# A two-layer spectral and convolution kernel: where the mix's matrix S is made, and how its operands are prepared

## The chip, the core and the metric

The kernel runs on one core of one Trainium2 chip. The metric is the device time of one execution in microseconds (us). The core has a matrix engine (TensorE, "PE", with its weight loads listed apart as "PEld"), a vector engine (VectorE, "DVE"), a scalar engine (ScalarE, "ACT"), GpSimd ("POOL") and SyncE ("SP"), which here only issues DMA transfers. The engines have their own instruction streams, taken in order, and wait for each other by semaphores. Operands lie in SBUF (128 partitions, also called lanes here); matmuls write to PSUM[...].

## The reference

Layer 0 is a Laplace neural operator on x (16 images, 16 channels, 256 x 256); layer 1 a small convolution network. Only layer 0's frequency part is touched:

```python
alpha = jnp.fft.fft2(x, axes=(-2, -1))
A = 1.0 / (omega1[:, None, None, None] - weights_pole1[None])
Bm = 1.0 / (omega2[:, None, None, None] - weights_pole2[None])
S = jnp.einsum('ikpq,oikp,xikq->oxik', weights_residue, A, Bm)
output_residue1 = jnp.einsum('biox,oxik->bkox', alpha, S)
...
x1 = jnp.fft.ifft2(output_residue1, s=(Ny, Nx), axes=(-2, -1)).real
```

S holds, for each of 256 x 256 frequencies (o, x), a complex 16 x 16 matrix from input channel i to output channel k. It factors: first sum over q with Bm (it depends on x only), then over p with A (it depends on o). Since x is real, only the row frequencies o = 0 to 128 are needed.

## The kernel before

The program has four stages, one after the other: `layer0_forward` (the transform of x, and beside it the making of tables), `layer0_mix` (the product with S, and the inverse transform along x), `layer0_back` (the inverse transform along y), and `layer1`.

**The forward stage** goes through 64 steps: 16 images (b) with 4 groups of 4 channels (cg). A step computes `rows` twice (16 matmuls into pu, L207, and 16 into pv, L214; the results leave PSUM through ACT's `right` L222 and DVE's `u` L224), then `poles` (L241), and from the second image on two or three calls of `columns` for the image before: each has two PSUM tiles px of 16 matmuls (L313), copied out by ACT (L320) and stored to `al` from GpSimd's queue (L329). Group norm's mean and variance are two tiny matmuls a step (L34, L42). The PSUM pools: psu 2 banks for pu, psv 2, psd 1, psx 2 for px, psn 1[...]. PE's order is written out by hand; the other engines' order is set by the scheduler.

At the end of each step from the fifth on (`i >= 4`), the generator `tables` is advanced by one piece. It makes three tables and stores them to DRAM from SyncE's queue: `td`, the sum over q (16 pieces: 6 DVE instructions for Bm, 8 for the weights, 4 matmuls L437 into a px bank, a copy L445 by ACT); `avd`, the values of A for each of the 33 groups of four row frequencies (11 pieces of three groups, 9 DVE instructions each, L466 to L490); and `ed`, exponentials for the back stage (16 pieces of some 25 DVE instructions and a sine on ACT, L515 to L536 and L769 to L783).

**The mix stage** goes through 33 groups g of four row frequencies; PE, ACT, DVE and POOL are ordered by hand. For a group:

- `poles` (L629, 6 DVE instructions) spreads the loaded A into block form `lt`; `residues` (L643) makes S: 16 k x 2 v x 2 h matmuls of `tt` (all of td, resident in SBUF) with `lt`, and copies each k from PSUM into `s` (L651 on DVE, L653 on ACT, half each). `s` is laid out [partition = (f, i), x, v, k], so these copies write elements that lie 64 bytes apart.
- `expand` (L605 on ACT, L607 on DVE) multiplies the loaded spectrum `alc` with one of four masks into `alb` [partition, x, j, b]; 16 instructions of 1024 elements a group (6 on ACT, 10 on DVE), writing elements 512 bytes apart.
- `mix` (L665) does 8 chunks of 32 small products, each chunk copied out of PSUM into `y` by ACT (L672). Four PSUM banks (psg) are for this and for `residues`.
- for each of the four frequencies f: `turn` (8 transposes L681, copied out as `yt` by DVE L687 and ACT L685) and `columns` (32 matmuls L700 into two banks `ph`; ACT copies the odd part L709, DVE adds and subtracts L712 and L713 to `h`, GpSimd issues the stores to `hd` L720). Between `turn` and `columns` of f stand four k of `residues` for the next group and a share of `expand`. `columns` of f = 3 is put off and runs in two halves between the chunks of the next group's `mix`.

`s`, `lt` and `alb` have one buffer each; the spectrum has four buffers of a quarter each, loaded by SyncE (L595) for the group after next as soon as a quarter has been expanded.

Of the kernel before, what the change touches and what calls it, by code (L numbers as in the profile page):

```python
# [10 lines left out]
F32 = mybir.dt.float32  # L11
# [61 lines left out]
def layer0_forward(ctx, tc, d, al, bd, tabs):  # L73
# [262 lines left out]
    with tc.manual_schedule(engines={mybir.EngineType.PE}):  # L336
# [4 lines left out]
        pieces = tables(ctx, tc, d, psx, tabs)  # L341
        acc = rsc = None
        for i, (b, cg) in enumerate(steps):
# [16 lines left out]
            if b:  # L360
                for g0 in range(8 * cg, 8 * cg + 8 if cg < 3 else NF, 4):
                    columns(b - 1, g0, rsc)
            if i + 2 < len(steps):
                fetched.append(fetch(*steps[i + 2]))
            if i >= 4:
                next(pieces, None)
# [16 lines left out]
def tables(ctx, tc, d, psum, tabs):  # L383

    nc = tc.nc
    td, avd, ed = tabs
# [3 lines left out]

    krow = load(nc, cp, d["krow_t"], [P, N], "krow_t")
    w = frequencies(nc, cp, d["tx"], krow, [P, N], "wt")
# [18 lines left out]
    for k in range(C):  # L411
        e = tp.tile([P, N], F32, tag="te", name="te")
        r = tp.tile([P, N], F32, tag="trec", name="trec")
        br = tp.tile([P, N], F32, tag="tbr", name="tbr")
# [7 lines left out]
        for h in range(2):  # L422
            wt = tp.tile([P, 2, 2, 16, M], F32, tag=f"wt{h}", name="wt")
            shape = [P, 16, M]
            for part, c, coef in ((0, 0, rr), (0, 1, ri), (1, 0, nri), (1, 1, rr)):
                nc.vector.tensor_tensor(
                    wt[:, part, c],
                    mt[:, h].unsqueeze(2).to_broadcast(shape),
                    coef[:, k].unsqueeze(1).to_broadcast(shape),
                    ALU.mult,  # L430
                )
            wts.append(wt)
        yield
        ps = psum.tile([P, 2, N], F32, tag="px", name="pt")
        for h, wt in enumerate(wts):
            for part, rhs in ((0, br), (1, e)):
                nc.tensor.matmul(  # L437
                    ps[:, h],
                    lhsT=wt[:, part].rearrange("p c i m -> p (c i m)"),
# [4 lines left out]
        t = tp.tile([P, 2, N], F32, tag="tt", name="tt")  # L444
        nc.scalar.copy(t, ps)  # L445
        nc.sync.dma_start(out=td[:, :, k], in_=t)

    krow = load(nc, cp, d["krow_m"], [P, N], "krow_m")  # L450
    w = frequencies(nc, cp, d["ty"], krow, [P, N], "wm")
    sign = load(nc, cp, d["sign_m"], [P, 1], "sign_m")
    pr = cp.tile([P, 32], F32, name="tpr")
    pi = cp.tile([P, 32], F32, name="tpi")
    for q in range(4):
        nc.sync.dma_start(out=pr[32 * q : 32 * q + 32], in_=d["p1r_ip"])
        nc.sync.dma_start(out=pi[32 * q : 32 * q + 32], in_=d["p1i_ip"])
    nc.vector.tensor_scalar(pi, pi, sign, None, ALU.mult)
    pr2 = cp.tile([P, 32], F32, name="tpr2")
    nc.vector.tensor_tensor(pr2, pr, pr, ALU.mult)  # L460
    npr = cp.tile([P, 32], F32, name="tnpr")
    nc.vector.tensor_scalar(npr, pr, -1.0, None, ALU.mult)
    for g in range(NF):
        four = [P, 32, 4]
        e = tp.tile(four, F32, tag="ae", name="ae")
        nc.vector.tensor_tensor(  # L466
            e,
            w[:, 4 * g : 4 * g + 4].unsqueeze(1).to_broadcast(four),
            pi.unsqueeze(2).to_broadcast(four),
            ALU.add,  # L470
        )
        r = tp.tile(four, F32, tag="ar", name="ar")
        nc.vector.tensor_tensor(r, e, e, ALU.mult)
        nc.vector.tensor_tensor(r, r, pr2.unsqueeze(2).to_broadcast(four), ALU.add)
        nc.vector.reciprocal(r, r)
        av = tp.tile([P, 32, 4, 3], F32, tag="av", name="av")
        half = [64, 32, 4]
        nprb = npr.unsqueeze(2)
        nc.vector.tensor_tensor(av[:64, :, :, 1], r[:64], nprb[:64].to_broadcast(half), ALU.mult)
        nc.vector.tensor_tensor(av[64:, :, :, 1], r[64:], e[64:], ALU.mult)  # L480
        nc.vector.scalar_tensor_tensor(
            av[:64, :, :, 0].rearrange("p k f -> p (k f)"),
            e[:64].rearrange("p k f -> p (k f)"),
            -1.0,
            r[:64].rearrange("p k f -> p (k f)"),
            ALU.mult,
            ALU.mult,
        )
        nc.vector.tensor_tensor(av[64:, :, :, 0], r[64:], nprb[64:].to_broadcast(half), ALU.mult)
        nc.vector.tensor_scalar(av[:, :, :, 2], av[:, :, :, 0], -1.0, None, ALU.mult)  # L490
        nc.sync.dma_start(out=avd[g], in_=av.rearrange("p k f l -> p (k f l)"))
        if g % 3 == 2:
            yield


    phase = load(nc, cp, d["phase"], [P, 1], "phase")
    turn = cp.tile([P, 1], F32, name="turn")
    nc.vector.tensor_scalar(turn, phase, TWO_PI, None, ALU.mult)
    last = load(nc, cp, d["last"], [P, 1], "last")
    c1 = 6.28125  # L500
    c2 = float(np.float32(TWO_PI - c1))
    for i, axis in enumerate("12"):
        pr = cp.tile([P, C], F32, name=f"epr{axis}")
        pi = cp.tile([P, C], F32, name=f"epi{axis}")
        for a in range(2):
# [1028 lines left out]
```

## Time and profile before

Three runs took 7180.24, 7201.38 and 7224.01 us (median 7201.38). The profiled execution took 7223.74 us, with a span of 7222.0 us between its first and last instruction.

| row of the profile | count | mean ns |
| --- | --- | --- |
| L437 PE, first factor of S | 128 | some 400 |
| L445 ACT copy tt, 128 x 512 from PSUM | 16 | 585 |
| L418 DVE reciprocal, 128 x 256 | 16 | 1742 |
| L518 DVE tensor_scalar, 128 x 512 in SBUF | 16 | 418 |
| L605 ACT expand, 128 x 1024 | 198 | 2055 |
| L607 DVE expand, 128 x 1024 | 330 | 1397 |
| L651 DVE, L653 ACT copies of S, 128 x 512 | 264 each | 1023, 1028 |
| L672 ACT copy y, L685 ACT copy yt | 264, 129 | 587, 586 |
| L536 SyncE store of ed, 256 KB | 16 | 338 (median) |
| L329 GpSimd store of al | 544 | 608 |

In the profile's lines, "out<-in" are the names of the tiles, "x2048" is a count, the numbers after the bar are the busy time of the whole group in us and the mean of one instruction in ns, and after the next bar stands the idle time of that engine just before these instructions and what ended it. Matmuls are pipelined, so a group's busy time divided by its count is what one costs, while its mean is from start to end. The clock (PEclk) is the share of full speed that TensorE was granted.

### The profile page before, as it was taken

Reading aid. Unit: us, or ns where it says so; the run is one execution under the profiler, and the core shown is the slowest. Engines: PE = TensorE matmul, PEld = TensorE weight load, DVE = VectorE, ACT = ScalarE, POOL = GpSimd, SP = SyncE. Lnnn points to the kernel's source line nnn. Section 1 sums busy time; section 2 is a strip of 40 time slices with the busy share of each in tenths; the row PEclk is TensorE's granted clock in tenths of the full one; section 3 lists DMA queues with packets and bytes.
Section 4 is the critical chain, followed back from the end, with each engine's and each line's share of the span. In section 5 each row is a group of like instructions: output and inputs, shape, how many; then the busy total and the mean of one; then the engine's idle time right before and its main releaser. Section 6 shows DMA issues by size and latency. Waiting matters only on the chain.

```text
span 7222.0 us, 144350 instructions
## 1 busy us (share of the span) xinstructions
PE 6585.2 (91%) x55592; PEld 3670.2 (51%) x55592; DVE 5553.1 (77%) x10106; ACT 3882.2 (54%) x6043; POOL 3517.7 (49%) x4614
## 2 busy tenths in 40 slices
PE   7889999889999999899789999999999999999996
PEld 5677778666666666677533333333333333333331
DVE  8999985466666666688688777878878787787875
ACT  2223333456656666222376666666666666666662
POOL 2334455322222222566664666556666566665563
PEclk9989999999999999999899999999999999999998
DMA  3444444433333333899878898898988888988886
GB/s 100 115 114 124 120 123 128 121 92 99 100 98 99 100 96 87 288 326 326 272 211 243 250 266 261 251 263 251 273 258 250 258 256 261 264 256 258 257 259 218
DMA packets 716081, 1443.39 MB, mean 200 GB/s; under 512 B 98954, under 2 KB 525254, under 8 KB 673638
## 3 DMA queue, kind: packets, MB, share of 16 engines
q1 hardware_dynamic: 567206, 959.76, 44.7%
q0 software_dynamic: 148192, 474.40, 21.9%
q8 instruction: 444, 7.27, 0.4%
q14 instruction: 239, 1.96, 0.1%
HBM read 877.12 MB, written 556.47 MB: 199 GB/s over the span
## 4 chain that ended last, share of the span: by engine, by line
PE 38%; DMA 7%; ACT 3%; DVE 1%; SPq 1%; issue 1%; POOL 0%; DVEq 0%; POOLq 0%; ACTq 0%
PE c2ps L1185 14%; PE c L1037 11%; PE pd L1105 11%; DMA rows<-cf 5%; ACT wide L1085 2%; DMA z<-zn 2%; PE pr L1064 2%; SPq L1017 0%; DVE top L1116 0%; ACT r L1073 0%; ACT L1240 0%; ACT L1085 0%; POOL o L1253 0%; DVE t L1113 0%; DVE pair L1175 0%
## 5 line engine op out<-in xcount | busy, mean ns | idle before, releaser
L1085 ACT ACTIVATE wide<-c,b 32x512 f32<-32x512 f32 x2176 | 1479.5, 680 | 295.1 <-PE c L1037 246.3
L1116 DVE TENSOR_TENSOR top<-pd,t 32x512 f32<-32x512 f32 x2176 | 1504.2, 691 | 55.6 <-DMA cf<-top 3.1
L1113 DVE TENSOR_TENSOR t<-pd,r 64x512 f32<-64x512 f32 x1088 | 744.4, 684 | 517.6 <-PE pd L1105 495.1
L1037 PE MATMUL c<-z,w 102*128 102x512 f32 x2048 | 1017.7, 629 | 122.9 <-ACT wide L1085 100.9
L1097 POOL COPY wide<-wide 32x1031 f32<-32x1031 f32 (+1 forms) x576 | 575.4, 999 | 1007.9 <-ACT wide L1085 980.5
L1105 PE MATMUL pd<-wide,dw 128*128 128x512 f32 x2048 | 993.4, 607 | 12.5 <-DVE top L1116 11.0
L720 POOL DMA_DIRECT2D hd<-h x512 | 324.3, 640 | 1206.8 <-DVE h L713 1182.0
L1185 PE MATMUL c2ps<-rows,c 128*32 128x512 f32 x6144 | 743.3, 617 | 100.8 <-DMA rows<-cf 96.1
L1037 PEld LDWEIGHTS c<-z,w 102*128 102x128 f32 x2048 | 377.8, 195 | 725.4 <-issue 475.5
L1105 PEld LDWEIGHTS pd<-wide,dw 128*128 128x128 f32 x2048 | 382.0, 192 | 573.8 <-issue 427.8
L1098 POOL COPY wide<-wide 32x1031 f32<-32x1031 f32 (+1 forms) x576 | 581.6, 1010 | 33.7
L1056 ACT ACTIVATE bot<-c,b 128x512 f32<-128x512 f32 x544 | 344.4, 684 | 470.7 <-issue 382.2
L700 PE MATMUL ph<-ix,yt 64*128 64x256 f32 x4128 | 505.3, 392 | 7.8 <-issue 7.1
L643 PE MATMUL ps<-tt,lt 128*64 128x256 f32 x4224 | 496.1, 385 | 13.1 <-DMA tt<-td 9.2
L1185 PEld LDWEIGHTS c2ps<-rows,c 128*32 128x32 f32 x6144 | 178.2, 110 | 622.5 <-issue 394.1
L313 PE MATMUL px<-wxn,u 128*64 128x256 f32 x4224 | 482.4, 380 | 7.9 <-ACT o L320 7.8
L207 PE MATMUL pu<-fy,eo 128*128 128x128 f32 x2048 | 425.7, 291 | 25.3 <-DVE u L224 21.1
L700 PEld LDWEIGHTS ph<-ix,yt 64*128 64x128 f32 x4128 | 395.1, 191 | 95.1 <-issue 47.2
L873 POOL TENSOR_TENSOR x<-x,o 128x512 f32<-128x512 f32 x256 | 324.4, 1267 | 217.8 <-DVE o L872 216.3
L607 DVE TENSOR_SCALAR alb<-alc,m 128x1024 f32<-128x1024 f32 x330 | 420.0, 1397 | 0.0
L214 PE MATMUL pv<-at,eo 128*128 128x128 f32 x2048 | 412.5, 285 | 0.0
L651 DVE COPY s<-ps 128x512 f32<-128x512 f32 x264 | 265.4, 1023 | 190.1 <-PE ps L643 172.5
(217 smaller groups left out, 11707.6 us busy)
## 6 DMA issues: line engine op xcount, KB each, us to landing
rows<-cf SPq DMA_DIRECT2D x128, 2176.0 KB
z<-zn SPq DMA_DIRECT2D x768, 257.8 KB
cf<-top POOLq DMA_DIRECT2D x512, 240.0 KB, 6.9
cf<-bot POOLq DMA_DIRECT2D x96, 840.0 KB, 11.6
alc<-al SPq DMA_DIRECT2D x264, 256.0 KB
zn<-zb SPq DMA_DIRECT2D x128, 516.0 KB
o<-zn SPq DMA_DIRECT2D x128, 516.0 KB
z<-in_x SPq DMA_DIRECT2D x64, 1024.0 KB
```

Of the source, the lines that this page charges most:

```text
L207: nc.tensor.matmul(pu[:, xh, e].rearrange("p v m -> p (v m)"), lhsT=lhs, rhs=fy[:, e], start=True, stop=True,)
L313: nc.tensor.matmul(ps[64 * k : 64 * k + 64, :, h], lhsT=u[:, h, part, g0 + j + k].rearrange("p f c -> p (f c)"), rhs=wxn[:, h, part], star ...
L643: nc.tensor.matmul(ps[64 * h : 64 * h + 64, v], lhsT=lt[:, h, k, 1 - v : 3 - v].rearrange("p l f c -> p (l f c)"), rhs=tt[:, h, k], start= ...
L700: nc.tensor.matmul(ph[q][:, e], lhsT=yt[lanes, i].rearrange("p t k -> p (t k)"), rhs=ix[lanes, i], start=n == 0, stop=n == 3,)
L1037: nc.tensor.matmul(ps[:, a], lhsT=w, rhs=z[:k, c : c + 2, 0:N], start=True, stop=True)
L1085: nc.scalar.activation(self.feat[64 - 32 * q : 96 - 32 * q, f, self.groups[g], :H], ps[q][32 * f : 32 * f + 32], AF.Mish, bias=b1[0][32 * ...
L1097: nc.gpsimd.tensor_copy(flat[0:32, f, 1:m], flat[64:96, f, 0 : m - 1])
L1098: nc.gpsimd.tensor_copy(flat[96:128, f, 0 : m - 1], flat[32:64, f, 1:m])
L1105: nc.tensor.matmul(ps, lhsT=dwt if self.tail else dw, rhs=self.feat[:, f, cs, :H], start=True, stop=True,)
L1113: nc.vector.tensor_tensor(t[64:128], ps[:64], self.r[:, cs], ALU.mult)
L1116: nc.vector.tensor_tensor(self.top[32 * f : 32 * f + 32, cs, q], ps[lanes], t[lanes], ALU.add)
L1185: nc.tensor.matmul(ps[32 * j : 32 * j + 32], lhsT=w[:, blk], rhs=src[:, 4 * j + blk : 4 * j + blk + 4, x : x + H], start=(i, blk) == (0, 0 ...
```

## The change

It moves the whole of S's making into the forward stage. `tables` now has two interleaved parts. `residues` takes the 16 k in pairs: `first` makes the sum over q as before (now kept in SBUF as `tt`); `second` makes A for 8 input channels and all 132 row frequencies at once (6 DVE and 8 ACT instructions) into `a`; `products` (16 groups of row frequencies at a time) and `last_products` (the last group) multiply the two by matmuls of 32 rows, in four PSUM banks, two from psx and two from psu; `evict` copies each bank to one of three SBUF buffers on ACT, and a store to the new DRAM table `sd` is issued from ACT's queue. The exponentials are as before, spread between. There are 128 pieces instead of 43; one is taken after the first `columns` of each step (and after g0 = 28), one at each step's end, from the second image on.

In the mix `poles`, `residues`, `tt`, `lt` and `avd` are gone. S of a group is loaded as `raw`, twice: as stored (v = 0) and with its two halves swapped (v = 1), three buffers of 2 MB. `prepare` makes `s` and `alb` for a range of 32 column frequencies. The spectrum is one tile of 2 MB with one buffer. The ranges of the next group are prepared behind the product chunks that used them: three inside `mix`, two after f = 0's `turn`, one after each of the others.

```diff
-        pieces = tables(ctx, tc, d, psx, tabs)
+        pieces = tables(ctx, tc, d, (psx, psu), tabs)
...
                     columns(b - 1, g0, rsc)
+                    if g0 in (8 * cg, 28):
+                        next(pieces, None)
...
-            if i >= 4:
+            if b:
                 next(pieces, None)
...
+    def second(k, h):
+        two = [P, 2, 132]
+        e = tp.tile(two, F32, tag="arg", name="ae")
...
+        for v in range(2):
+            t = tp.tile(two, F32, tag="n" if v else "exp_b", name="ax")
+            for j in range(2):
+                nc.scalar.activation(
+                    t[:, j],
+                    e[:, j],
+                    AF.Identity,
+                    bias=xc[:, v, h, k + j : k + j + 1],
+                    scale=xs[:, v : v + 1],
+                )
+            nc.vector.tensor_tensor(t, t, r, ALU.mult)
+            for c in range(2):
+                nc.scalar.activation(
+                    a[:, :, c, :33, v],
+                    t.rearrange("p k (g f) -> p k g f", f=4),
+                    AF.Copy,
+                    scale=mc[:, c : c + 1],
+                )
+
+    def banks():
+
+        return [
+            (psx if r < 2 else psu).tile([P, 2, N], F32, tag="px" if r < 2 else "pu", name="s")
+            for r in range(4)
+        ]
+
+    def evict(ps, n=P):
+        t = tp.tile([P, 2, N], F32, tag="s", name="s", bufs=3)
+        nc.scalar.copy(t[:n], ps[:n])
+        return t.rearrange("p k x -> p (k x)")
+
+    def products(k, tt, h, c, g0):
+
+        ps = banks()
+        for j in range(2):
+            for r in range(4):
+                q = slice(32 * r, 32 * r + 32)
+                nc.tensor.matmul(
+                    ps[r][:, j],
+                    lhsT=a[q, j, c, g0 : g0 + 16].rearrange("p g v f -> p (g v f)"),
+                    rhs=tt[q, h, j],
+                    start=True,
+                    stop=True,
+                )
+        for r in range(4):
+            dst = sd[g0 : g0 + 16, :, :, 8 * h + 2 * r + c, k : k + 2]
+            nc.scalar.dma_start(out=dst.rearrange("g v f k x -> (g v f) (k x)"), in_=evict(ps[r]))
...
+    rp = ctx.enter_context(tc.tile_pool(name="mr", bufs=3))
+
+    def load_residues_of(g, v):
+
+        t = rp.tile([P, C, N], F32, tag="raw", name="raw")
+        for lanes, part in ((slice(0, P), None),) if v == 0 else ((slice(0, 64), 1), (slice(64, P), 0)):
+            src = sd[g] if part is None else sd[g, part : part + 1]
+            nc.sync.dma_start(
+                out=t[lanes].rearrange("p k x -> p (k x)"),
+                in_=src.rearrange("v f c k x -> (v f c) (k x)"),
+            )
+        return t
...
+    def load_spectrum(g):
+
+        t = gp.tile([P, nb, 2, P], F32, tag="alc", name="alc")
+        nc.sync.dma_start(
+            out=t.rearrange("p b e x -> p (b e x)"),
+            in_=al[g].rearrange("v p b x -> (v p) (b x)"),
+        )
         return t
...
+    def prepare(raw, t, i):
+
+
+        xs = slice(32 * i, 32 * i + 32)
+        nc.vector.tensor_scalar(
+            s[:, xs, 0], raw[0][:, :, xs].rearrange("p k x -> p x k"), sg, None, ALU.mult
+        )
+        nc.scalar.copy(s[:, xs, 1], raw[1][:, :, xs].rearrange("p k x -> p x k"))
+        src = t[:, :, :, 16 * i : 16 * i + 16].rearrange("p b e x -> p x e b")
+        for j in range(4):
+            dst = alb[:, xs, j].rearrange("p (x e) b -> p x e b", e=2)
+            if j == 0 or (j == 1 and i % 2):
+                nc.scalar.activation(dst, src, AF.Copy, scale=m4[:, j : j + 1])
             else:
+                nc.vector.tensor_scalar(dst, src, m4[:, j : j + 1], None, ALU.mult)
...
             nc.scalar.copy(y[:, :, x0 : x0 + 8], ps.rearrange("p x j -> p j x"))
+            if x0 in (16, 32, 48):
+                next(then, None)
...
+            then = operands(raw, spectrum) if more else iter(())
+            mix(y, between, then)
+            if g + 2 < NF:
+                following = [load_residues_of(g + 2, 0)]
             for f in range(4 if more else 1):
                 yt = turn(y, f)
...
+                for _ in range(2 if f == 0 else 1):
+                    next(then, None)
+                if f == 3 and g + 2 < NF:
+                    raw = following + [load_residues_of(g + 2, 1)]
+                    spectrum = load_spectrum(g + 2)
                 between = columns(g, f, yt)
```

## The prediction

> **What bounds the kernel now.** I read the windows by stage first (columns: stretch, length, then busy time of PE, PEld, DVE, ACT, POOL with instruction counts, granted clock, DMA share, GB/s), then the groups of instructions in the mix's steady part, then PE's waits in the forward transform, then short windows around the start of the mix and around one gap of PE.
>
> ```profile
> 0.00:1375.00 1375.00, 1225.72 (x11040) 998.30 (x11040) 1107.99 (x3039) 436.83 (x802) 587.06 (x810) 0.97 0.42 116
> 1375.00:2914.00 1539.00, 1386.16 (x26280) 1052.96 (x26280) 1017.30 (x1436) 937.64 (x1113) 327.43 (x514) 0.98 0.34 99
> ...
> 1500.00:2800.00 1300.00, 1187.83 (x22354) 901.27 (x22346) 867.91 (x1232) 798.31 (x952) 283.48 (x448) 0.98 0.34 97
> ```
>
> The change touches only the forward transform (to 1375) and the mix (1375 to 2914). TensorE (PE) is busy 89% and 90% there, with DVE second. In the forward stage DVE works 792 of 860 us between 180 and 1040, where the tables are made, and PE is idle 92 us of them; from 1040 to 1370, without tables, PE is never idle.
>
> ```profile
> L700 PE MATMUL ph<-ix,yt 64*128 64x256 f32 x3584 | 440.9, 393 | 7.1 <-issue 7.1
> L643 PE MATMUL ps<-tt,lt 128*64 128x256 f32 x3584 | 419.5, 383 | 3.9 <-issue 2.9 <-ACT y L672 1.0
> L665 PE MATMUL pg<-alb,s 128*32 128x64 f32 x14290 | 236.5, 223 | 101.2 <-issue 60.7 <-DVE s L651 40.1
> L681 PE MATMUL pt<-ident,y 128*128 128x128 f32 x896 | 122.5, 280 | 0.0
> ```
>
> 896 transposes at 32 a group are 28 groups in 1300 us: 46.4 us a group, of which PE works 43.6: L700 15.75, L643 15.0 (S made anew), L665 8.45 (the products), L681 4.4. In PE's waits of 180 to 1370 only the tables' DVE work shows:
>
> ```profile
> PE gn_var L42 <- DVE gnq L39: 61.0, 21, 5.3
> PE pu L207 <- DVE u L224: 20.8, 23, 1.9
> PE px L313 <- ACT o L320: 7.8, 5, 1.9
> ```
>
> Two prices come from short windows. A 128-lane load (tt, ix) runs at 409 to 418 GB/s; the 64-lane loads of alc that follow, at about 182. And PE, idle for 4.5 us at 1546, comes back at half clock and keeps it about 5 us.
>
> ```profile
> 1380.00:1385.00 5.00, 5.00 (x26) 3.14 (x24) 1.01 (x1) 1.33 (x2) 0.00 (x0) 0.50 1.03 418
> 1390.00:1395.00 5.00, 5.00 (x50) 3.61 (x48) 2.89 (x4) 3.06 (x3) 0.00 (x0) 1.00 0.60 182
> ...
> 1549.00:1551.00 2.00, 0.53 (x21) 0.53 (x24) 0.00 (x0) 0.00 (x0) 0.00 (x0) 0.50 0.03 5
> 1553.00:1555.00 2.00, 2.00 (x12) 1.28 (x8) 0.00 (x0) 0.00 (x0) 0.00 (x0) 0.50 0.00 0
> 1557.00:1559.00 2.00, 2.00 (x103) 1.84 (x93) 0.00 (x0) 1.36 (x3) 0.00 (x0) 1.00 0.04 8
> ```
>
> [...]
>
> **The mix, part by part.** Removed per group: L643's 128 matmuls (15.0 us of PE), 16 evictions of 1.02 us, half on DVE and half on ACT, and 6 L629 of 0.68 on DVE. The expansion of the spectrum goes from 10 DVE x 1.40 and 6 ACT x 2.06 to 20 DVE and 12 ACT instructions of half the size, with 8 more on each for S. None of these shapes is in the trace. Below: 512 elements without penalty, 0.42 us on DVE (L518) and 0.59 on ACT (L685); above: twice that, as L651 and L653 with scattered writes, 1.02. I take 0.65 and 0.9. DVE then has 28 x 0.65 + 9.4 (h and yt) = 27.6 us a group and ACT 20 x 0.9 + 9.8 = 27.8: neither is the bound.
>
> Were nothing else in the way, a group would take 33.8 us. From the end of the transposes of f = 3 (call it T): products and the halves of columns between them, 8.45 + 4.0 of PE and about 1.1 for ACT's last copy of y, 13.5; then for f = 0 transposes 1.1, yt 0.8, columns 3.7; for f = 1 and 2, 6.8 each, since columns wait for odd, four h and yt of DVE (in the timeline transposes start at 1520.8 and yt is ready at 1523.7), which L643 filled before; and 1.1 for the last transposes: 20.3.
>
> But the loads are in the way. Group g+1's operands are finished at f = 3; only then do the one buffer of the spectrum and the third raw buffer come free. In the program built from the changed code SyncE's loads for g+2 wait for just that: the swapped raw half for ACT's S copy of range 7 (T + 1.6 us), the spectrum for DVE's and ACT's last expansion (T + 4). The first preparation, which needs both, stands in DVE's and ACT's order behind the third chunk of products, and everything later on those engines stands behind it: the copies of y, odd, h, yt. Only 4 PSUM buffers let PE go on, to T + 11.5. The swapped half is two 64-lane loads of 1 MB at about 200 GB/s, 10.5 us[...], then 2 MB at 415, 5 us; with 1 us to start, about 1 to land and 1 for the hd writes between, the spectrum is there at T + 14 to T + 20. I take 18.5. From there ACT has one expansion, five copies of y, two odd and five preparing instructions before the transposes: 0.9 + 5 x 0.59 + 0.65 + 5 x 0.9 = 9.0 us. PE, idle for more than 4.5 us twice, then runs about 5 us at half clock: + 2.5. Sum: 18.5 + 9.0 + 2.5 + 20.3 = 50.3 us, against 46.4. So the 15 us that leave PE are eaten by a load that nothing covers. 32 groups x 3.9 = +125. At the start the first products (1409 before) can begin as soon as range 0 is prepared, near 1390, the eight ranges still to be made: -15. Mix: +110; between -190 (T + 13, ACT chain 7.6, warm clock: 41 us a group) and +300 (56 us).
>
> **The forward transform.** Gone: 33 avd steps, some 127 us of DVE (rows L466 to L490) and 33 SyncE stores. The 16 first-factor tables stay (L437's 64 matmuls, L418). New, 16 times: a second factor of 6 DVE instructions (reciprocal of 264 elements by L418's 1742 ns for 256, five at 0.43: 3.95, in all 63 us) and 8 on ACT; the exponentials keep their work. New, 64 times: 8 matmuls into four PSUM banks, and 16 times 16 smaller ones. By L700's rate they take 60 ns each or less, some 40 us of PE in all. The banks cost more. Two are columns' px, two are rows' pu, and all four are emptied by ACT (0.585 as L445), with a store issued from ACT after each: no ACT store is in the trace, so I take 0.34 us (SyncE's ed stores of the same shape, 338 ns[...]). A call between two columns: the second bank waits for columns' last eviction (0.9), matmuls (0.6), then the next columns wait for the first eviction (0.8): 2.3 us. A call at a step's end: 1.5, then the next rows' pu waits for two evictions, two issues and a third eviction: 2.6, in all 4.1. PE has nothing else in its order. Queued behind these on ACT are o, right and v, and through right DVE's u. With 44 calls of the first and 36 of the second kind: 101 + 148 = 249 us. Against it DVE has 64 us less to do where it holds PE: -64. Forward: +185; if the banks are hidden in waits that exist anyway, +30; if also the three store buffers and the second factor's chain through ACT hold PE, +270.
>
> S's stores, 33 x 2.1 = 69 MB beside the 160 MB (1375 us at 116 GB/s) that the forward stage moves at a DMA share of 0.42, I take as hidden; uncovered they would lengthen stores and with them the waits for the three store buffers, which the +270 holds. Start-up tables and constants, SBUF addresses, the back transform and layer 1: unchanged, nothing.
>
> **Sum.** The profiled execution has span 7222.0 and 7223.7 in all. + 185 + 110 = 7519; the median of the runs is 0.3% below the profiled execution (7201.4), so 7495.
>
> **Rivals.** A, faster: the loads come early (halves side by side) and strided reads cost nothing: a group at 41 us, mix -190, forward +50: 7223.7 - 140 = 7084, or 7060 by the median. For it: DMA share is only 0.34 in the mix, PE is its bound. Against: the wait lists and 182 GB/s. It decides where load plus ACT chain stay below 46.4 - 20.3 = 26 us. B, no change: mix -110 and forward +110, 7200. C, much slower: strided reads at twice the price on both engines and loads slowed by the stores, 56 us a group, and forward +250: 7223.7 + 550, 7750. D, that it does not do what it says (the operands waiting for all products, not by range): against it, ACT's first preparation waits in the built program for the loads and nothing of PE beyond the chunk before; it would give C's time.
>
> **Numbers.** Likeliest, 0.56, 7300 to 7650. A 0.22, B 0.06, C and D 0.16. The range of 8 in 10: 7060 to 7720. About 0.5% is what a measurement here can tell from no change: faster 0.22, same 0.06, slower 0.72.
>
> **What would show it.** In the mix: ACT's first S copy or expansion of each group waiting for DMA for over 5 us, PE idle about 8 us twice a group with clock 0.5 after, some 50 us a group. In the forward stage: pu waiting for ACT's copy of s, some 80 times. I am wrong if the spectrum lands by T + 11 (then no wait), or if forward stays near 1375.

## The result, and the profile after

The changed kernel took 7833.79 us (median of 4 runs, 7825.2 to 7849.06), the kernel before 7200.57 (4 runs, 7180.24 to 7224.01): 1.0881 times as long, with a 95% interval of 1.0843 to 1.0918. The profiled execution has a span of 7823.4 us against 7222.0, 601.4 more. The prediction had the sign and both places, and half of the size.

Where the time went shows in the windows by stage (columns as before: stretch, length, busy time of PE, PEld, DVE, ACT, POOL, granted clock, DMA share, GB/s):

```profile
0.00:1743.00 1743.00, 1454.38 (x12576) 1131.41 (x12576) 1097.77 (x2837) 658.13 (x1249) 580.53 (x806) 0.92 0.43 124
1743.00:3534.00 1791.00, 1102.36 (x22056) 926.42 (x22056) 821.83 (x1565) 999.34 (x1310) 310.35 (x516) 0.78 0.51 156
```

The forward transform's last matmul now starts at 1742.6, the mix's first product at 1773.6 (before: 1409.0) and its last matmul of `columns` at 3533.6 (before: 2909.2). So 365 us were lost up to the first product and 260 in the mix from there (1500 to 1760); the rest of the program took 23 less. In the mix PE works 1102 us, some 280 less than before, as the change meant, but it stands idle for 690 of 1791, and its clock is 0.78. (Some of the counts of matmuls given ahead are records of the trace: the 32 of `columns` in the mix are 16 matmuls of the program, which leave two records each.)

The groups of instructions of PE in the forward transform (180 to 1748):

```profile
L313 PE MATMUL px<-wxn,u 128*64 128x256 f32 x4096 | 489.5, 386 | 39.2 <-ACT s L512 31.5 <-ACT o L320 7.7
L207 PE MATMUL pu<-fy,eo 128*128 128x128 f32 x1856 | 423.3, 315 | 140.2 <-ACT s L512 80.9 <-DVE u L224 43.0 <-DVE gnv L44 9.6
L214 PE MATMUL pv<-at,eo 128*128 128x128 f32 x1856 | 406.8, 306 | 0.0
L521 PE MATMUL s<-tt,ta 32*128 32x256 f32 x1024 | 119.9, 424 | 38.6 <-ACT o L320 25.5 <-ACT ta L496 9.4 <-ACT s L512 2.8
L539 PE MATMUL s<-tt,ta 32*32 32x256 f32 x512 | 29.4, 401 | 10.9 <-ACT o L320 9.9 <-ACT s L512 1.0
```

The products themselves (L521, L539) take 149 us of PE. `pu` and `px` wait 112 us for ACT's copies of the product banks (L512), where they waited for nothing of the kind before. And `rows`' matmuls L207 and L214, which had 291 and 284 ns, have 315 and 306: a part of them runs at half clock (granted clock 0.50 from 1164 to 1170, in the call below; 0.92 in the whole stage, 0.97 before). ACT itself waits before these copies, for a store of S to free one of the three SBUF buffers:

```profile
ACT s L512 <- DMA sd<-s: 120.8, 79, 3.8
```

One call and what follows, in PE's timeline (start, length, group, idle time before it):

```profile
1160.41 0.69 PE L521 MATMUL s<-tt,ta 32*128 32x256 f32 x2
1161.27 1.14 PE L521 MATMUL s<-tt,ta 32*128 32x256 f32 x14 [0.16 <-ACT o L320]
1162.34 0.38 PE L34 MATMUL gn_mean<-mv,ones 128*128 128x2 f32 x2
1164.23 0.80 PE L207 MATMUL pu<-fy,eo 128*128 128x128 f32 x2 [1.51 <-ACT s L512]
1164.82 0.63 PE L214 MATMUL pv<-at,eo 128*128 128x128 f32 x2
...
1170.30 0.39 PE L207 MATMUL pu<-fy,eo 128*128 128x128 f32 x2
```

After a wait of 1.51 us, pairs of records that take 0.39 us at full clock take 0.63 for the next 6 us, at a granted clock of 0.50.

In the mix, 885 records of the transposes L735 between 1900 and 3400, at 32 a group, are 27.7 groups: 54.2 us a group. The waits of that stretch (engine, what it waited with and for, us in all, times, longest):

```profile
DVE alb L704 <- DMA alc<-al: 505.7, 28, 19.5
ACT s L697 <- DMA raw<-sd: 320.1, 28, 12.6
ACT alb L702 <- DMA alc<-al: 113.0, 28, 5.0
PE pg L717 <- issue: 203.3, 55, 8.1
PE pt L735 <- ACT y L724: 160.4, 28, 6.6
```

DVE stands 18 us in every group before an expansion, for the spectrum; ACT 15, for the swapped raw half and then the spectrum. One group with T (the end of the last transposes) at 2324.7, in windows:

```profile
2326.00:2332.00 6.00, 5.04 (x216) 4.20 (x204) 2.61 (x5) 4.15 (x6) 1.57 (x3) 1.00 0.78 200
2332.00:2341.00 9.00, 3.25 (x106) 3.08 (x108) 0.00 (x0) 0.00 (x0) 0.00 (x0) 0.62 0.99 244
2341.00:2346.00 5.00, 3.04 (x80) 2.23 (x78) 0.00 (x0) 1.08 (x1) 0.00 (x0) 1.00 1.01 426
2346.00:2356.00 10.00, 2.23 (x66) 1.99 (x67) 7.38 (x14) 9.48 (x13) 2.36 (x4) 0.59 0.40 154
2356.00:2378.00 22.00, 18.12 (x181) 15.35 (x182) 14.54 (x30) 15.08 (x21) 5.49 (x9) 0.88 0.22 64
```

From 2332 DVE and ACT do nothing; the two 64-lane loads run at some 240 GB/s together with stores of hd (q1 alone moved 2.39 MB from 2329 to 2340, 217 GB/s), then, from 2341, the spectrum, of 128 lanes, at 426. At 2346.2 (T + 21.5) it is there. Then ACT works through its order for 9.5 us while PE mostly waits (2.2 of 10 us busy), and only in the last 22 us does PE run most of the time. What moved between 2326 and 2340 is told by the queues (packets, MB, share): q1 holds SyncE's loads, q0 GpSimd's stores of hd.

```profile
q1 hardware_dynamic: 183, 2.49, 74.4%
q0 software_dynamic: 320, 0.53, 15.9%
```

### The profile page after: what moved, and what is told of

Its sections match the earlier page's. It is cut to its first block, busy times and chain, and to the rows that moved or that the text cites. A ratio compares the mean times of both kernels' runs of the same rounds, so it can differ in the third digit from the quotient of the medians.

```text
span 7823.4 us, 139730 instructions
## 1 busy us (share of the span) xinstructions
PE 6531.8 (83%) x52904; PEld 3675.5 (47%) x52904; DVE 5352.4 (68%) x10038; ACT 4163.1 (53%) x6689; POOL 3493.4 (45%) x4615
## 4 chain that ended last, share of the span: by engine, by line
PE 55%; DMA 16%; ACT 12%; DVE 12%; issue 4%; SPq 1%; POOL 1%; ACTq 0%; DVEq 0%; POOLq 0%
PE c2ps L1232 13%; PE c L1084 11%; PE pd L1152 10%; DMA alc<-al 7%; ACT alb L702 5%; PE px L313 4%; DMA rows<-cf 4%; PE pu L207 2%; PE ph L754 2%; PE pv L214 2%; ACT wide L1132 2%; PE pr L1111 2%; ACT s L697 2%; PE py L907 2%; DMA sd<-s 2%
## 5 line engine op out<-in xcount | busy, mean ns | idle before, releaser
L774 POOL DMA_DIRECT2D hd<-h x512 | 308.3, 609 | 1475.6 <-DVE h L767 1452.0
L704 DVE TENSOR_SCALAR alb<-alc,m 128x512 f32<-128x512 f32 x660 | 427.2, 699 | 592.8 <-DMA alc<-al 592.8
L754 PE MATMUL ph<-ix,yt 64*128 64x256 f32 x4128 | 612.6, 453 | 138.7 <-DVE yt L741 102.5
L717 PE MATMUL pg<-alb,s 128*32 128x64 f32 x16896 | 338.4, 244 | 366.4 <-issue 229.5
L754 PEld LDWEIGHTS ph<-ix,yt 64*128 64x128 f32 x4128 | 491.2, 228 | 230.8 <-ACT yt L739 151.1
L207 PE MATMUL pu<-fy,eo 128*128 128x128 f32 x2048 | 462.6, 312 | 142.6 <-ACT s L512 80.9
L702 ACT ACTIVATE alb<-alc,m 128x512 f32<-128x512 f32 x396 | 476.8, 1238 | 136.5 <-DMA alc<-al 136.5
L313 PE MATMUL px<-wxn,u 128*64 128x256 f32 x4224 | 503.9, 386 | 39.2 <-ACT s L512 31.5
L717 PEld LDWEIGHTS pg<-alb,s 128*32 128x32 f32 x16896 | 301.7, 126 | 411.2 <-issue 266.3
L697 ACT COPY s<-raw 128x512 f32<-128x512 f32 x264 | 290.1, 1099 | 378.6 <-DMA raw<-sd 378.6
```

What stands on the lines that cost most here:

```text
L207: nc.tensor.matmul(pu[:, xh, e].rearrange("p v m -> p (v m)"), lhsT=lhs, rhs=fy[:, e], start=True, stop=True,)
L313: nc.tensor.matmul(ps[64 * k : 64 * k + 64, :, h], lhsT=u[:, h, part, g0 + j + k].rearrange("p f c -> p (f c)"), rhs=wxn[:, h, part], star ...
L702: nc.scalar.activation(dst, src, AF.Copy, scale=m4[:, j : j + 1])
L717: nc.tensor.matmul(ps[32 * q : 32 * q + 32, x], lhsT=s[:, i].rearrange("p v k -> p (v k)"), rhs=alb[:, i].rearrange("p j b -> p (j b)"), s ...
L754: nc.tensor.matmul(ph[q][:, e], lhsT=yt[lanes, i].rearrange("p t k -> p (t k)"), rhs=ix[lanes, i], start=n == 0, stop=n == 3,)
```

## The experiments

A group's time below is always 1000 us (window 1900 to 2900) divided by a 32nd of the transposes' records there (54.8 by this count for the changed kernel, 54.2 by the longer window above, which is used); the end of the forward transform is told by the mix's first product, which follows its last matmul by some 31 us. The forward code of e1, e2, e6, e7, e10 and e12 is the changed kernel's, and their first products came between 1763 and 1784: so much it varies by itself. e1, e3, e4, e5, e7, e8, e9 and e12 ran once each, the others four or five times.

**e1: no loads after group 1.**

```diff
-            if g + 2 < NF:
-                following = [load_residues_of(g + 2, 0)]
...
-                if f == 3 and g + 2 < NF:
-                    raw = following + [load_residues_of(g + 2, 1)]
-                    spectrum = load_spectrum(g + 2)
```

> Leaves out the mix's loads from group 2 on: every later group is prepared again from group 1's raw tiles and spectrum, so the later groups' results are not those of their frequencies. The forward transform is untouched. Theory 1 (the loads that nothing covers stop ACT, and with it PE, twice a group): no DMA wait is left on ACT and DVE, PE's half clock goes with the idle time, a group falls from 54.2 us to 36 to 40, the mix to some 1250 to 1350 us, the whole to 7270 to 7400. Theory 2 (ACT's 20 strided instructions at 1.1 to 1.24 us set the pace, 30 us of ACT in PE's way): a group stays at 46 us or more, the whole at 7570 or more.

7321.66 us. PE's groups, and the window:

```profile
L717 PE MATMUL pg<-alb,s 128*32 128x64 f32 x13465 | 215.9, 220 | 33.0 <-issue 32.6
L735 PE MATMUL pt<-ident,y 128*128 128x128 f32 x864 | 124.2, 289 | 73.4 <-ACT y L724 73.4
```

```profile
1900.00:2900.00 1000.00, 777.40 (x17753) 665.46 (x17753) 669.13 (x1283) 802.42 (x1063) 260.53 (x429) 0.94 0.21 59
```

864 records are 27 groups: 37.0 us each, clock 0.94. ACT and DVE do all their work of preparation and still a group is 17 us shorter. The loads, not ACT's instructions, make the 54.2; theory 2 is out. ACT is now the busiest engine (802 of 1000, PE 777); whether 37.0 can be undercut no run shows.

**e2: the same loads by halves.**

```diff
-        t = rp.tile([P, C, N], F32, tag="raw", name="raw")
+        t = rp.tile([P, C, P], F32, tag=f"raw{v}{h}", name="raw")
...
-        t = gp.tile([P, nb, 2, P], F32, tag="alc", name="alc")
+        t = gp.tile([P, nb, 2, P], F32, tag="alc", name="alc", bufs=2)
...
+                if f in (0, 3) and g + 2 < NF:
+                    raw[f // 3] = [load_residues_of(g + 2, v, f // 3) for v in range(2)]
```

> The mix with the same loads, the same SBUF and nothing left out: each raw tile is two tiles of 128 columns with one buffer each, so the first half is loaded as soon as range 3 is prepared (behind f = 0) and the second as soon as range 7 is; the freed third raw buffer becomes a second buffer of the spectrum, which is loaded a whole group ahead. Theory 1: the loads are covered, a group takes 37 to 43 us (6.3 MB of loads and 2.1 MB of hd writes in it, 200 GB/s or more), the whole 7300 to 7480. If the 64-lane loads of the second half (issued at T, needed at f = 0's range 4, some 17 us later) still come late: 44 to 48 us, 7520 to 7650. Theory 2 (ACT): 46 us or more with no DMA wait in front of ACT.

7589.05 us, 1.0532 [1.0512, 1.0553] of before: 3% better than the changed kernel, with nothing left out, but a group is 46.0 us (696 records), not 37 to 43. The number alone would also suit theory 2; the waits do not. PE's:

```profile
PE pg L719 <- issue: 165.7, 50, 7.0
PE ph L756 <- DVE yt L743: 77.4, 44, 3.0
PE pt L737 <- ACT y L726: 34.0, 22, 2.4
```

No engine waits for a load any more. Instead PE stands 7.6 us a group (165.7 / 21.75) in the middle of the products, with nothing in the profile to wait for; in e1 it was 1.2. One such gap lies from 2310.9 to 2317.3, and the DMA view of just that stretch (queue: packets, MB, share) shows a packet of the instruction queue among the loads (a packet counts whole where it starts, so a share can pass 100%):

```profile
q1 hardware_dynamic: 2802, 1.42, 121.1%
q8 instruction: 1, 0.02, 1.1%
```

That gave a new theory: PE's own instructions come late when loads fill the DMA engines. The packet records of the traces agree with it. Queue q8, which the profile names "instruction", moves packets of 16,384 bytes, one for every 250 to 260 records of PE and PEld together (98 packets between 1900 and 2900 in the changed kernel, 139 in e1, 113 in e2). Between 1900 and 2900 PE stands over 1.5 us before a product, with "issue", 24 times in the changed kernel, 30 in e2, 30 in e5, 24 in e10, 2 in e1. In every one of these gaps a packet of q8 ends, and PE starts 1.2 to 1.9 us after it; of all starts of products in these windows only 14 to 24% lie 1.2 to 2.0 us behind one.

**e5: loads that nothing waits for.** The kernel of e1 with the loads put back into a tile that nothing reads.

```diff
-                following = [load_residues_of(g + 2, 0)]
+                load_residues_of(g + 2, 0, unused)
...
-                    raw = following + [load_residues_of(g + 2, 1)]
-                    spectrum = load_spectrum(g + 2)
+                    load_residues_of(g + 2, 1, unused)
+                    load_residues_of(g + 2, 0, unused)
```

> The kernel of e1 (every group after the first prepared from group 1's tiles) with loads of the left-out sizes, 6.3 MB a group, put back at their places in the program, but into a tile that nothing reads: no engine waits for them. Theory 6 (what was left in e2, 7.6 us a group of PE waiting for 'issue' in the products, is PE's instructions being fetched behind the loads): PE pg <- issue comes back from 1.2 to 5 to 9 us a group, and a group goes from 37.0 to 42 to 46 us though nothing waits for a load. Theory 7 (the issue waits of e2 belong to its order of work, not to the loads): a group stays at 37 to 39 us and issue at 1 to 2.

7492.76 us. PE's groups:

```profile
L719 PE MATMUL pg<-alb,s 128*32 128x64 f32 x11584 | 209.3, 233 | 123.6 <-issue 123.5
L737 PE MATMUL pt<-ident,y 128*128 128x128 f32 x728 | 109.2, 298 | 47.6 <-ACT y L726 47.6
```

728 records: 44.0 us a group instead of 37.0, though no instruction depends on these loads. For the same reason SyncE ran ahead of the groups with them: 9.2 MB a group instead of 6.3 (172.47 MB in 18.75 groups) until some 2750, then none. So the run holds its own counter-test, from 1900 to 2750 with loads and from 2800 to 3090 without:

```profile
L719 PE MATMUL pg<-alb,s 128*32 128x64 f32 x9536 | 176.8, 235 | 118.7 <-issue 118.6
L737 PE MATMUL pt<-ident,y 128*128 128x128 f32 x600 | 89.9, 298 | 35.8 <-ACT y L726 35.8
...
L719 PE MATMUL pg<-alb,s 128*32 128x64 f32 x3712 | 59.1, 220 | 10.1 <-issue 10.1
L737 PE MATMUL pt<-ident,y 128*128 128x128 f32 x248 | 37.4, 299 | 22.1 <-ACT y L726 22.1
```

600 and 248 records: 45.3 us a group with 6.3 of waiting for issue, then 37.4 with 1.3. ACT's and DVE's instructions are no slower beside the loads (the expansions 1223 and 698 ns, in e1 1232 and 699). So with these loads, which nothing waits for, a group is some 8 us longer here. How the 17.2 us by which a changed group is longer than one without loads divide into this and the waiting for loads is not shown: in the changed kernel the gaps (203.3 us of issue, 7.3 a group) fall in part into the wait for the spectrum, as from 2332 to 2337.7 in the group above. The profile does not say which instruction a packet held.

**e6 and e10: the loads moved away from the products.**

```diff
-                for _ in range(2 if f == 0 else 1):
+                for _ in range((2, 2, 1, 0)[f]):
                     next(then, None)
-                if f in (0, 3) and g + 2 < NF:
+                if f in (0, 2) and g + 2 < NF:
...
-    with tc.manual_schedule(engines={E.PE, E.Activation, E.DVE, E.Pool}):
+    with tc.manual_schedule(engines={E.PE, E.Activation, E.DVE, E.Pool, E.SP}):
```

(Against e2's kernel; in both, the spectrum is also loaded at f = 0, behind the first halves. The last two lines are e10's alone.)

> The kernel of e2 with ranges 5 and 6 prepared behind f = 1 and range 7 behind f = 2, so that the second halves are loaded from f = 2 instead of T on, and the spectrum behind the first halves instead of at T: the loads then run beside columns (16 matmuls of PE in 2 us) instead of beside the products (64 in 1 us). Theory 6: PE pg <- issue falls from 7.6 to 2 to 4 us a group, a group takes 39 to 43 us, the whole 7380 to 7510. Theory 7 (the order, or DMA's own limit at 8.4 MB a group): 45 to 48 us, 7560 to 7650.

> The kernel of e6 with SyncE's loads in the order that the program writes: in e6's trace the spectrum was issued behind the second halves, at some 6 us into the group, and so still came beside the products. Here: first halves, spectrum, second halves. Theory 6 (PE's instructions wait behind loads): issue waits of pg fall from 6.3 to 3 to 5 us a group, a group from 46.0 to 41 to 44 us, the whole 7430 to 7530. If 25 us of loads cannot be kept off the products whatever the order: 45 to 47 us, 7560 to 7610.

e6: 7580.64 us, 1.0505 [1.0485, 1.0524], 46.0 us a group: a miss, and no test of the theory, since SyncE's queue had the spectrum behind the second halves, beside the next products (issued at 2349.5 in a group whose products begin at 2346.6; in e10 at 2328.1, 15 us ahead of them). e10, with the order that was meant: 7513.81 us, 1.0444 [1.0424, 1.0464], 760 records, so 42.1 us a group (in its fastest execution, 7482.57, which is the profiled one). PE's waits of e10:

```profile
PE ph L756 <- DVE yt L743: 89.7, 44, 3.0
PE pg L719 <- issue: 85.5, 35, 5.6
```

Issue fell to 3.6 us a group and the group by 3.9. From the first to the last product of a group, in the mean of the window's groups, the DMA engines were 91% busy in e2 (5.0 MB), 75% in e6 (4.4 MB) and 61% in e10 (2.5 MB), and PE waited 7.6, 6.3 and 3.6 us for issue: fewer loads beside the products, less waiting there.

**e12: the swapped half as one load over 128 lanes.**

```diff
-        for lanes, part in ((slice(0, P), None),) if v == 0 else ((slice(0, 64), 1), (slice(64, P), 0)):
+        for lanes, part in ((slice(0, P), None),):
```

> The changed kernel with the swapped raw half loaded by one load over 128 lanes in the order of the first one, instead of two over 64 lanes each; the same bytes. The two parts of S's second half are then exchanged, so the results are not the reference's. Theory 10 (a load of 64 lanes runs at half rate and the two do not run beside each other, 10 us instead of 5): the spectrum lands some 5 us earlier behind T, DVE's wait for alc falls from 18 to 12 to 14 us a group, a group from 54.2 to 48 to 51, the whole to 7650 to 7730. If the rate in that stretch (211 to 260 GB/s) is that of loads and hd writes together and not of the lanes: 53 us or more, the whole at 7790 or more.

7646.06 us, and 672 records: 47.6 us a group. The waits, to be set beside the 18.1 and 11.4 us a group (505.7 and 320.1 over 28) of the changed kernel:

```profile
DVE alb L704 <- DMA alc<-al: 253.8, 20, 13.7
...
ACT s L697 <- DMA raw<-sd: 115.1, 20, 7.2
```

12.7 and 5.8 us: the same bytes arrive 5.5 us earlier. As two loads of 64 lanes they moved at 217 GB/s in the group shown above, where the spectrum, one load over 128 lanes, had 426 (before: 182 and 418). That cost this kernel 6 to 7 us a group, 188 us in all (7833.79 less 7646.06).

**e7: ACT reads without strides.** Both kinds of ACT's preparing instructions read other elements, in runs; what they write stays in its place.

```diff
-        nc.scalar.copy(s[:, xs, 1], raw[1][:, :, xs].rearrange("p k x -> p x k"))
+        nc.scalar.copy(s[:, xs, 1], raw[1][:, 2 * i : 2 * i + 2].rearrange("p k (x c) -> p (k x) c", c=C))
...
-                nc.scalar.activation(dst, src, AF.Copy, scale=m4[:, j : j + 1])
+                flat = t[:, 2 * i : 2 * i + 2].rearrange("p b e x -> p (b e x)")
+                nc.scalar.activation(
+                    alb[:, xs, j], flat.rearrange("p (x b) -> p x b", b=nb), AF.Copy, scale=m4[:, j : j + 1]
+                )
```

> ACT's 20 preparing instructions of a group read their 512 elements in runs instead of with strides (other elements of the same tiles, so the mix's operands are not the reference's); writes, counts and loads as they are. If strided reads are what makes them 1.10 to 1.24 us, each falls to 0.6 to 0.7. Theory 1 (a group is load plus ACT's chain): the chain from landing to the transposes falls from 9.5 to 6 or 7 us, a group from 54.2 to 50 to 52, the whole to 7690 to 7770. Theory 2 (ACT sets the pace): 44 us or less, 7500 or less. If the writes are the price, nothing changes.

7699.67 us, 640 records: 50.0 us a group. ACT's groups, changed kernel first:

```profile
L702 ACT ACTIVATE alb<-alc,m 128x512 f32<-128x512 f32 x221 | 266.3, 1239 | 73.3 <-DMA alc<-al 73.3
L697 ACT COPY s<-raw 128x512 f32<-128x512 f32 x148 | 162.8, 1100 | 219.8 <-DMA raw<-sd 219.8
```

```profile
L703 ACT ACTIVATE alb<-alc,m 128x512 f32<-128x512 f32 x240 | 165.8, 724 | 93.3 <-DMA alc<-al 93.3
L697 ACT COPY s<-raw 128x512 f32<-128x512 f32 x160 | 100.0, 625 | 231.8 <-DMA raw<-sd 231.8
```

The stride of the read is the price: 1239 ns become 724, and 1100 become 625. ACT's 20 instructions, some 10 us cheaper a group, are worth 4.2 us as long as the loads hold it.

**e3, e9 and e4: what the products cost the forward transform.** e3 leaves out matmuls, banks and copies; e9 leaves out the copies alone (both store a fixed tile); e4 runs each matmul over 128 rows.

```diff
+    fixed = tp.tile([P, 2, N], F32, name="s")
...
-            nc.scalar.dma_start(out=dst.rearrange("g v f k x -> (g v f) (k x)"), in_=evict(ps[r]))
+            nc.scalar.dma_start(out=dst.rearrange("g v f k x -> (g v f) (k x)"), in_=fixed)
```

```diff
-                    lhsT=a[q, j, c, g0 : g0 + 16].rearrange("p g v f -> p (g v f)"),
-                    rhs=tt[q, h, j],
+                    lhsT=a[:, j, c, g0 : g0 + 16].rearrange("p g v f -> p (g v f)"),
+                    rhs=tt[:, h, j],
```

> Leaves out the products of the forward transform: no matmuls of 32 rows, no evictions, no PSUM banks taken from columns and rows; the factors are still made, and every store of S is still issued from ACT, of the same size and to the same place, from one fixed tile. S is then not the reference's. Theory 1 (matmuls 149 us, waits for ACT's copies 150 us, the half clock after them 90 us): the forward transform ends at 1400 to 1480 instead of 1750, clock 0.97 or more, the whole at 7480 to 7570. Theory 3 (ACT's store issues of 0.33 us and 69 MB of stores beside the reads are what holds it): it ends at 1600 or later, the whole at 7680 or more. The mix stays at 54 us a group either way.

> Leaves out ACT's copies of the four banks in the forward transform: the 32-row matmuls run as changed and take their banks in turn, but nothing reads them, and every store of S is issued from one fixed tile as in e3 (end of the forward transform there 1369, with the products 1743). S is not the reference's. Splits the 374 us. Theory 8 (the matmuls' own time, 149 us, and the half clock that their 32 rows bring by themselves, some 100): clock 0.92 to 0.94, the forward transform ends at 1580 to 1640. Theory 9 (the half clock needs PE's wait after the call as well): clock 0.97 or more without the waits, the end at 1500 to 1550. If the waits for ACT were most of it: before 1480.

> Each of the eight matmuls of a products call runs over all 128 rows instead of one tile of 32 rows, so S sums four poles' products and is not the reference's; the same banks, copies and stores. Asks why rows run at half clock (0.64 instead of 0.39 us a matmul) for some 5 us after a call although PE was idle only 1.5 us. Theory 4 (32-row tiles count as little work for the clock): the rows stay at full clock, forward clock 0.96 or more against 0.92, L207 and L214 together back from 830 to some 770 us, and the forward transform shorter by 0 to 60 us although the products themselves cost more. Theory 5 (the gap itself): clock 0.92 or below, L207 and L214 as before, the forward transform longer by 20 to 100 us.

The first product of the mix came at 1401.1 in e3, at 1624.5 in e9 (1773.6 changed), and the whole took 7462.28, 7677.13 and, for e4, 7840.31 us. In e3 every store of S is still issued from ACT and the forward transform ends where it did before (last `columns` at 1369.2 against 1370.0): the 69 MB of stores and their issues cost nothing as long as no copy waits for their buffers, and the products, with these waits, cost all 372 us. e9 splits these: 149 go with the copies, 223 stay with the matmuls, of which 148 are their own busy time. The 149 hold the three store buffers too: ACT's 120.8 us of waiting for them go with the copies, and in the changed kernel 6.8% of the chain that ended last from 180 to 1370, some 81 us, is the landing of these stores. Copies and buffers are not told apart; no run has more buffers.

That e3 ends no earlier than before, with less table work on DVE, is seen in PE's waits of 180 to 1370 in e3:

```profile
PE pu L207 <- DVE u L224: 42.2, 29, 2.6
PE px L313 <- ACT o L320: 17.4, 15, 2.6
PE gn_var L42 <- DVE gnq L39: 10.3, 10, 5.0
PE pd L241 <- ACT v L231: 9.6, 7, 4.2
```

Before, they were 20.8, 7.8, 61.0 and none: the wait in front of `gn_var` went, and most of it came back elsewhere.

The windows of 180 to 1370 in the order e3, e9, e4 give the clock (0.92 in the changed kernel):

```profile
180.00:1370.00 1190.00, 1093.62 (x10194) 890.38 (x10188) 932.53 (x2500) 447.54 (x856) 546.77 (x758) 0.98 0.54 159
```

```profile
180.00:1370.00 1190.00, 1062.36 (x9794) 834.94 (x9796) 817.18 (x2207) 376.69 (x722) 447.32 (x616) 0.95 0.49 143
```

```profile
180.00:1370.00 1190.00, 1047.42 (x8804) 832.60 (x8806) 762.97 (x1998) 475.63 (x909) 401.27 (x555) 0.98 0.45 131
```

e9 lies between the two theories: without the waits for the copies, the calls of 32-row matmuls still cost some clock, but half as much. In e4 the calls are followed by waits too (0.8 us instead of 1.5 in the call shown) and the clock is that of e3, while L521 takes 260.7 us instead of 119.9. L313, L207 and L214 together take 1320 us changed, 1263 in e9, 1236 in e4, 1220 in e3. So of the 372 us, 100 are these matmuls' slower running (1320 less 1220), of which e9 keeps 43. Clock and matmul time were exchanged in e4, and the whole is the changed kernel's within 0.1%; that it would be shorter was a miss. What e4 cannot separate is the height of the rows from the shorter wait.

**e8 and e11: two engines for the copies.**

```diff
-        nc.scalar.copy(t[:n], ps[:n])
+        if r % 2:
+            nc.vector.tensor_copy(t[:n], ps[:n])
+        else:
+            nc.scalar.copy(t[:n], ps[:n])
```

> In the forward transform DVE copies every second bank of products, ACT the others; all else as changed. Theory 1 (PE waits for ACT's copies of the four banks, 161 us of it): pu, px and s waiting for L512 fall to 50 to 90 us, the forward transform ends 40 to 110 us earlier than 1743, and the half clock behind the calls stays (0.91 to 0.93). If DVE's own work in the way (u, the tables) makes its copies late, the end moves by less than 30 us or later.

> The mix of e10 and the two engines' copies of e8 together, nothing left out. If both act by themselves, e10's time less 15 to 35 us; slower than before (7200) in any case, since the forward transform alone has lost some 350 us.

e8: 7808.64 us, first product at 1747.3, 26 us earlier than in the changed kernel and 16 than the earliest that has the changed kernel's forward code: by itself unclear. e11 took 7486.45 us, 1.0389 [1.0373, 1.0406] against e10's 1.0444 [1.0424, 1.0464], some 27 us in the median. But in the profiled executions (7485.50 and 7482.57) the first product of the mix comes at 1763.5 in e11 and at 1763.4 in e10. So that two engines shorten the forward transform is not shown. In e8 PE waits 86 us for ACT's copies and 31 for DVE's, in all no less than the 116 of the changed kernel: the waits moved. Those for the three buffers are now mostly DVE's:

```profile
DVE s L513 <- DMA sd<-s: 80.6, 37, 4.4
```

e11 is the best of the variants that leave nothing out, and slower than the kernel before.

## Why the prediction came out half as large

Two parts of the sum failed. The forward transform was put at + 185 and lost 372, by a matmul count in the wrong unit, a clock that was left out and a relief that did not come. A group of the mix was put at + 3.9 us and lost 7.8, by a spectrum that landed too late. Point by point, with the working on record above:

- **Forward, the matmuls: the step that failed first.** "60 ns each or less, some 40 us of PE in all": that matmuls of 32 rows take half of the 123 ns of L700's of 64 (440.9 us over 3584) was an estimate that no trace of before showed, and L700's rate was per record of the trace, and a matmul of the program leaves two (L700's 4128 are 2064 matmuls). The 768 new matmuls are 1536 records (1024 of L521 and 512 of L539), which doubles the sum; and in calls as short as 16 records the first two take 0.69 us, so that a record came to 97 ns overall (117 in L521). 149 us instead of 40: + 109.
- **Forward, the banks: right in kind, too dear.** 2.3 and 4.1 us a call contain 0.6 of matmul; the waiting in them is 44 x 1.7 + 36 x 3.5 = 201 us. With the copies go 149 in e9, of which 57 are the slower running of L313, L207 and L214. The place stands (pu waiting for ACT's copy of s, 46 times where "some 80" were named, and px as often). The three store buffers, which the prediction kept for its + 270, did hold ACT.
- **Forward, the half clock: missing.** The prediction priced it in the mix alone. e9's 223 us less the 148 of the matmuls leave 75: 43 for slower matmuls, the rest for the products' own and other waits. With the 57 above, the slower running is some 100 us.
- **Forward, "-64 for DVE's relief": nothing came.** e3 has all of the lighter tables and ends at the same point as before (- 1). Up to 1370 DVE works 1076 us there against 1107, 30 less instead of 64, and PE's waits came back at other places, as shown with e3. Sum, with e3 as the middle: 149 + 149 + 75 - 1 = 372, against + 185.
- **Mix, the mechanism: right.** Single buffers, the load behind range 7, ACT's order behind the load, PE idle twice (5.8 and 5.7 us in the group shown, where "about 8" was named): e1 shows that without the loads 17 us a group go, and a group is 37.0 where the prediction had 33.8. Sizes of the one group shown: the spectrum at T + 21.5 instead of 18.5; ACT's chain 9.5 instead of 9.0; half clock and the rest, by subtraction, 23.2 instead of 22.8. Sum 54.2 instead of 50.3. The mis-sized term is the landing. The prediction's own parts add up to 1.6 + 1 + 10.5 + 5 + 1 + 1 = 20.1 (1 to start and 1 to land were estimates; the `bd` stores of before, L292, take 1.8 us at least from issue to landing); it took 18.5, as if the two 64-lane loads needed less than the 10.5. At q1's 217 GB/s of 2329 to 2340 they need about that (2.1 MB in 9.7 us), and only as one load (e12) did the same bytes come 5.5 us earlier. "1 for the hd writes between" was too little as well: 0.53 MB of hd went between, which at the stretch's 217 GB/s (q0 and q1 together, 2326 to 2340) is an estimated 2.4 us. That gives 21.5. Over 32 groups the 3.9 us missing are + 125 us.
- **Mix, prices of ACT and DVE.** DVE's 0.65 was 0.70; ACT's 0.9 was 1.10 and 1.24 (e7: the strided read). It cost little, because the chain holds only six of the twenty.
- **Start of the mix:** "- 15" was - 8 (1401.1 in e3 against 1409.0).
- **Rivals.** A's condition (an early load) is e12 and e1: 47.6 us with whole loads, 37.0 with none, against the 41 that it named. C comes nearest in the mix (56 us): strided reads were dear on ACT, and hd stores slowed the loads; but the waiting was for loads. D is out: with the loads gone the operands do follow by ranges behind the products.

## What to carry to other kernels

Before moving work off the busiest engine, ask whether the loads it covered still find cover: here 15 us of matmuls went out of each group while its loads grew from 2.3 to 6.3 MB, and with single buffers that come free only at a group's end the saving turned into a wait. Count a trace's records and a program's instructions in the same unit before multiplying a rate with a number. And price short bursts of narrow matmuls with what follows them: the emptying of their banks, the buffers that the copies need, and the clock of the full matmuls behind. Here 149 us of such matmuls, with their copies and stores, made the forward transform 372 longer.

## What was not expected of the hardware

- **PE stood longer beside loads that it does not wait for.** With few loads it waited for "issue" before products 1.2 us a group in e1 and 2.2 before the change (60.7 over 28 groups), beside many 6.3 in e5 while its loads ran and 7.6 in e2, in single gaps of up to 7.8. In every gap over 1.5 us between 1900 and 2900 of the changed kernel, e1, e2, e5 and e10 (24, 2, 30, 30 and 24 of them) a packet of queue q8, "instruction", ends.
- **Half clock came after a short wait.** Before the change it was seen after 4.53 us of idle PE (1550 to 1554: 0.50). The changed forward transform shows it after 1.51 us idle behind 1.8 us of 32-row matmuls (0.63 us a pair instead of 0.39, for 6 us, clock 0.50), and not after 0.80 us behind 128-row ones (e4: 0.39 us a pair); whether the rows' height or the length of the wait made the difference is not shown.
- With its loads in rows of 512 bytes e2 kept the DMA engines 77% busy for 182 GB/s (1900 to 2900), the changed kernel 51% for 157 (1900 to 3400).
